# Half-size products in another order, channels split into chunks 0, 2 and 1, 3, norm by halves, and scores on 32 by 64 tiles

## The chip, the cores and the metric

The kernel runs on one core of one Trainium2 chip. The time is that of the device in microseconds, from the start of the program to its end. Engines are named as in the profile: PE is TensorE's matmuls and PEld its weight loads, DVE is VectorE, ACT is ScalarE, POOL is GpSimd, and SP, ACT and POOL also issue DMA transfers.

## The reference

The input `x` holds eight images of 32 by 32 positions with 512 channels, in fp32. Two attention layers follow each other, each with a group norm ahead of it and a residual around it:

```python
# N = 1024 positions, C = 512 channels, for each of 8 images
x = x + L0(gn(x))      # gn: 32 groups of 16 channels, mean and variance over positions and group
x = x + L1(gn(x))

def L0(xn):            # 16 heads of 32 channels
    q, k, v = split(xn @ w_qkv)
    return softmax(q * 32**-0.5 @ k.T) @ v @ w_proj + b_proj

def L1(xn):            # 4 heads of 128 channels
    q, k, v = xn @ Wq * 128**-0.5, xn @ Wk, xn @ Wv
    return softmax(q @ k.T + relative_position_logits(q, pos_emb_w, pos_emb_h)) @ v @ Wo
```

## The kernel before

Activations lie transposed in SBUF: a block has 128 partitions, four chunks of 128 channels (`CC` = 4) and 1024 positions, which are worked on in two halves of 512 (`NB`). A chunk is `xT[cc]`.

**Projections by seven products.** Each 512 by 512 projection is computed as a 2 by 2 block product with seven half-size products instead of eight (the Winograd form of Strassen's scheme). The activations' quarters are a11, a12 (first 512 positions), a21, a22 (last 512); the channels are cut into chunks 0, 1 (a11, a21) and 2, 3 (a12, a22). `forms` (L320) makes the four sums of quarters on DVE: s1 = a21 + a22, s2 = s1 - a11, a11 - a21 (in place of a21) and s4 = a12 - s2. The weights' quarters and sums are cut alike: `quarter` (L120), `Matrix.add_up` (L131, sums at L142, stored in DRAM). `seven` (L337) runs the products of one unit, half of the output channels, in the order P1, P6, P2, P5, P7, P3, P4 (indices 0, 5, 1, 4, 6, 2, 3 of `ORDER`, L161, which also sets the order in which `Stream` fetches weights). They add up in three PSUM banks, x, y and z; P1 and P7 are copied out by ACT as `p1` and `p7`, `a` (L368) and `b` (L376) are sums that DVE makes between two products into y, and a sink then makes the four results: `Plain` writes them, `Onto` adds them to the residual. Every product is issued by `by_columns` (L301), four matmuls of 32 output columns side by side. Unit u gives output chunks u and u + 2.

**Group norm.** `statistics` (L238) gathers mean and variance of a chunk on DVE into the tile `mv`; `group_norm` (L250) takes all four chunks at once: a 32 by 32 transpose, group averages, deviations, and back, about nine small DVE operations (L256 to L281), a power by POOL for 1/sqrt (L285), and then four DVE passes over the chunks (L288), in place. `put_away` stores the chunks as they were ahead of the norm, and `fetch` brings them back for the residual.

**Attention of layer 0** (`attention_0`): steps over groups of four heads m, halves of queries h and blocks of 128 keys j. A front (L525) computes the scores of four heads of 32 channels, each 128 keys by 512 queries, on four row tiles of TensorE, into the four banks of the one PSUM tile `ps`; ACT takes the exponential into `e` (L533, two buffers). A back (L544) adds the values, four heads side by side in columns, and DVE sums the `e` of all key blocks (L553, L555). `finish` and `normalise` divide by the row sums (DVE L493 to L509, POOL L513).

```python
for r in range(HB):                       # L522: HB = 4 heads
    rows = slice(r * D0, (r + 1) * D0)    # D0 = 32
    nc.tensor.matmul(ps[:, r, :], k[m][rows, j * P : (j + 1) * P],
                     q[m][rows, h * NB : (h + 1) * NB], start=True, stop=True)
```

**Attention of layer 1** (`attention_1`): steps over heads, halves and key blocks, with 128 by 128 matmuls (L640, L641, L652); heads in the order 0, 1, 2, 3.

**Order of the work.** The images overlap. While layer 0's attention of image b runs, `side_by_side` puts between its steps the output projection of layer 0 of image b - 1 (`after_0`, weights `w_p`), that of layer 1 of image b - 2 (`after_1`, `w_o`) with the norm of image b - 1 woven in, layer 1's projections (`second`, `w_q`, `w_k`, `w_v`) and attention of image b - 1, and the projections of image b + 1. Where there is no image b - 2, in the second round, the norm has nothing beside it: it is given `ALONE` steps, in which attention goes on by itself. A planner sets the final order of instructions on each engine from there. `load_first` brings the first image by matmul transposes; the weights' sums of the first three matrices are made around it.

Of the kernel before, what the change touches and what calls it, by code (L numbers as in the profile page):

```python
# [27 lines left out]
def quick_path(  # L28
# [68 lines left out]
    neg_half = consts.tile([P, CC], F32, tag="neg_half", name="neg_half")  # L97
# [22 lines left out]
    def quarter(w, i):  # L120
        k, n = i // 10 - 1, i % 10 - 1
        return w[:, k * HC : (k + 1) * HC, n * HN : (n + 1) * HN]

    class Matrix:

# [6 lines left out]
        def add_up(self, engine, queue, store, keep=False):  # L132

            t = block(f"prep_{self.name}")
            whole = t[:, : CC // 2, :].rearrange("p a (b n) -> p (a b) n", n=NB)
            sums = t[:, CC // 2 :, :].rearrange("p a (b c n) -> p (a b) c n", c=HC, n=HN)
            queue.dma_start(whole, self.w)
# [23 lines left out]
    ORDER = [0, 5, 1, 4, 6, 2, 3]  # L161
# [47 lines left out]
    def put_away(xT, name):  # L209
        kept = []  # L210
        for cc in range(CC):
            d = dram.tile([P, N], F32, tag="kept", name=f"d_{name}_{cc}", bufs=4 * CC)
            nc.sync.dma_start(d, xT[cc])
            kept.append(d)
        return kept
# [21 lines left out]
    def statistics(st, xT, cc, name):  # L237

        if "mv" not in st:
            st["mv"] = small.tile([P, 32], F32, tag="mv", name=f"mv_{name}", bufs=2)  # L240
            nc.gpsimd.memset(st["mv"], 0.0)
        s = small.tile([P, NH, 6], F32, tag="st", name=f"st_{name}_{cc}", bufs=2)
        for h in range(NH):
            nc.vector.bn_stats(s[:, h, :], xT[cc][:, h * NB : (h + 1) * NB])
        nc.vector.bn_aggr(
            st["mv"][:, : 2 * CC].rearrange("p (s c) -> p c s", c=CC)[:, cc, :],
# [3 lines left out]
    def group_norm(st, xT, name, after=None):  # L250

        mv = st.pop("mv")
# [16 lines left out]
        with tc.issue_after(after().ins) if after is not None else nullcontext():  # L269
# [9 lines left out]
        mean = back[:, 0, :CC]  # L279
        var = small.tile([P, CC], F32, tag="var", name=f"var_{name}")  # L280
        nc.vector.scalar_tensor_tensor(  # L281
            var, back[:, 0, CC : 2 * CC], GN_EPS, back[:, 1, :CC], op0=ALU.add, op1=ALU.add
        )
        rstd = small.tile([P, CC], F32, tag="rstd", name=f"rstd_{name}")
        nc.gpsimd.tensor_tensor(rstd, var, neg_half, op=ALU.pow)  # L285
        yield 0
        for cc in range(CC):
            nc.vector.tensor_scalar(  # L288
                xT[cc],
                xT[cc],  # L290
                mean[:, cc : cc + 1],
                rstd[:, cc : cc + 1],
                op0=ALU.subtract,
                op1=ALU.mult,
            )
            if cc % 2:
                yield 0
# [22 lines left out]
    def forms(x, name):  # L320


        a11, a12 = x[:, :HC, :NB], x[:, HC:, :NB]
        a21, a22 = x[:, :HC, NB:], x[:, HC:, NB:]
        s1, s2, s4 = [
            mem.tile([P, HC, NB], F32, tag=f"form{i}", name=f"f{i}_{name}", bufs=1) for i in (1, 2, 4)
        ]
        nc.vector.tensor_add(s1, a21, a22)  # L328
        nc.vector.tensor_sub(s2, s1, a11)  # L329
        nc.vector.tensor_sub(a21, a11, a21)  # L330
        nc.vector.tensor_sub(s4, a12, s2)
        return [a11, a12, s4, a22, s1, s2, a21]
# [4 lines left out]
    def seven(fs, u, rows, sink, name, hook=None):  # L337
# [26 lines left out]
        yield HC  # L364
        y = bank(f"y_{name}")
# [13 lines left out]
        z = bank(f"z_{name}")  # L379
        product(z, 6, True)  # L380
        p7 = snapshot("e1", f"p7_{name}")
        nc.scalar.copy(p7, z)  # L382
# [3 lines left out]
        if hook is not None:  # L386
            hook()
        yield HC
        product(z, 3, False)
        sink.c21(z, a)  # L390
        sink.c22(b, p7)
# [76 lines left out]
    def project_rows(fs, m, y, name, hook=None):  # L468

        for u in range(2):  # L470
# [11 lines left out]
                hook if u else None,  # L482
# [32 lines left out]
    def attention_0(q, k, v, b):  # L515
# [4 lines left out]
        def front(m, h, j):  # L520
            name = f"0_{b}_{m}_{h}_{j}"
            ps = psum.tile([P, HB, NB], F32, tag="ps", name=f"ps_{name}", bufs=1)  # L522
            for r in range(HB):
                rows = slice(r * D0, (r + 1) * D0)
                nc.tensor.matmul(  # L525
                    ps[:, r, :],
                    k[m][rows, j * P : (j + 1) * P],
                    q[m][rows, h * NB : (h + 1) * NB],
                    start=True,
                    stop=True,  # L530
                )
# [98 lines left out]
    def attention_1(q, k, v, posT, b):  # L630

        steps = [(h, c, j) for h in range(H1) for c in range(NH) for j in range(NT)]
# [56 lines left out]
    def load(b, st):  # L689
# [17 lines left out]
        st["kept"] = put_away(xT, f"0_{b}")  # L707
        yield from group_norm(st, xT, f"0_{b}")
# [3 lines left out]
    def load_first(st):  # L712

        rows = block("x_rows", [P, NT, C])
        for t in range(NT):
            queue = nc.scalar if t % 2 else nc.sync
            queue.dma_start(rows[:, t, :], xf[0, t * P : (t + 1) * P, :])
        x = block("x0T_0")
        xT = chunks(x)
        for h in range(NH):  # L720
# [13 lines left out]
            for cc in range(CC):  # L734
                part = xT[cc][:, h * NB : (h + 1) * NB]
                if h == 0 or cc % 2:
# [3 lines left out]
        for cc in (1, 0, 3, 2):  # L740
            statistics(st, xT, cc, "0_0")
        st["kept"] = put_away(xT, "0_0")
        run(group_norm(st, xT, "0_0"))
# [18 lines left out]
    def before_0(b, st, hook=None):  # L762
# [10 lines left out]
    def after_0(b, st, hook=None):  # L773
# [3 lines left out]
        xT = fetch(st["kept"], x)  # L777
        for u in range(2):
# [3 lines left out]
                fs, u, False, Onto(halves(xT, u), bias), f"wp_{b}_{u}", hook if u else None  # L782
# [4 lines left out]
    def norm_1(b, st, after=None):  # L787
        xT = chunks(st["x1"])
        st["kept"] = put_away(xT, f"1_{b}")
        yield from group_norm(st, xT, f"1_{b}", after)  # L790

    def second(b, st):
# [12 lines left out]
            keys_and_values, position_logits(q, posT, b), 2, len(ORDER), (0, 1, 2)  # L805
# [3 lines left out]
    def forms_1(b, st):  # L809
        st["ao1"] = forms(st["ao"], f"ao1_{b}")  # L810

    def after_1(b, st, hook=None):

        if "ao1" not in st:
            forms_1(b, st)
        fs = st.pop("ao1")
        xT = fetch(st["kept"], block(f"x2T_{b}"))
# [637 lines left out]
```

## Time and profile before

| | |
|---|---|
| time, median of 3 runs | 3914.23 us (3910.26 to 3914.39) |
| profiled run, span | 3913.0 us, mean clock of TensorE 0.993 |
| PE idle before its first products (11.4 to 24.8 us) | 13.4 us |
| ACT exponential of four heads, L533 | 512 of 1.88 us |
| DVE row sums of layer 0, L555 and L553 | 384 of 2.31 us, 64 of 2.74 us |
| DVE sum of quarters (one of four of `forms`) | 1.2 us, more beside POOL |
| POOL multiply of `normalise`, L513 | 128 of 1.67 us |

In the profile, a line of a group gives the source line, engine and operation, the tile written and the tiles read, the shape (for TensorE first rows times columns of the array in use), how often, then busy time and mean duration, then the idle time of the engine ahead of these instructions and what ended it. TensorE's matmuls overlap, so their durations don't add up to time; what counts is from one group's start to the next.

### The profile page before, as it was taken

The numbers are of one execution on the slowest core, as the hardware profiler recorded it, in microseconds if no ns is written. First come the engines' busy times: TensorE is split into PE (matmuls) and PEld (weight loads), VectorE is DVE, ScalarE is ACT, GpSimd is POOL, SyncE is SP. The second block draws the span as 40 slices with busy tenths as digits, with TensorE's granted clock in tenths as the row PEclk, the third lists the DMA queues.
The fourth block names the chain that finished last, engine by engine and source line by source line (L and its number), as shares of the span: only waits on it lengthen the run. The fifth ranks groups of instructions, "written<-read, shape, count | busy, mean of one in ns | idle before, by whom it ended". The sixth has DMA issues, their size and how long they took to land. (4 is left out here: it accounts for less than half of the span.)

```text
span 3913.0 us, 71616 instructions
## 1 busy us (share of the span) xinstructions
PE 3820.3 (98%) x30370; PEld 1414.5 (36%) x30370; DVE 2518.9 (64%) x2905; ACT 1726.1 (44%) x1767; POOL 620.7 (16%) x400
## 2 busy tenths in 40 slices
PE   7999899999999999999999999999999999999998
PEld 3222244232443234432343323433234332344353
DVE  5777675576745867468664686656865568754544
ACT  2554553445434454344544445344453445543132
POOL 1341001121101211012111121111200112011101
PEclk8999999999999999999999999999999999999999
DMA  5231120133201322023120241103311122110401
GB/s 168 74 108 50 41 60 3 39 117 70 59 5 63 106 56 55 12 90 84 44 54 17 91 94 39 44 24 97 88 44 32 30 91 68 32 63 18 124 17 23
DMA packets 482952, 234.21 MB, mean 60 GB/s; under 512 B 269600, under 2 KB 461376, under 8 KB 481600
## 3 DMA queue, kind: packets, MB, share of 16 engines
q1 hardware_dynamic: 470464, 212.69, 20.0%
q0 software_dynamic: 2608, 13.70, 0.9%
q8 instruction: 242, 3.96, 0.4%
q10 hardware_dynamic: 9552, 3.15, 0.4%
q14 instruction: 86, 0.70, 0.1%
HBM read 170.72 MB, written 58.72 MB: 59 GB/s over the span
## 5 line engine op out<-in xcount | busy, mean ns | idle before, releaser
L533 ACT ACTIVATE e<-ps 128x2048 f32<-128x2048 f32 x512 | 962.1, 1879 | 844.8 <-PE ps L525 650.1
L555 DVE TENSOR_TENSOR es<-es,e 128x2048 f32<-128x2048 f32 x384 | 888.7, 2314 | 405.6 <-ACT e L533 403.5
L525 PE MATMUL ps<-q,k 32*128 32x512 f32 x4096 | 591.3, 642 | 33.7 <-ACT e L533 33.6
L643 ACT ACTIVATE e<-ps 128x512 f32<-128x512 f32 x512 | 305.9, 598 | 585.8 <-PE ps L641 549.4
L544 PE MATMUL acc<-e,v 128*32 128x512 f32 x4096 | 549.5, 608 | 0.4 <-ACT su L491 0.4
L640 PE MATMUL ps<-q,k 128*128 128x512 f32 x1024 | 523.6, 593 | 0.4 <-DVE posT L626 0.4
L652 PE MATMUL acc<-e,v 128*128 128x512 f32 x1024 | 521.9, 592 | 0.0
L513 POOL TENSOR_TENSOR q<-q,su 128x512 f32<-128x512 f32 x128 | 214.2, 1673 | 1568.2 <-DVE su L509 1567.5
L663 DVE TENSOR_TENSOR es<-es,e 128x512 f32<-128x512 f32 x384 | 291.7, 760 | 264.5 <-ACT e L643 263.2
L641 PE MATMUL ps<-posT,sel 128*128 128x512 f32 x512 | 406.7, 794 | 0.0
L525 PEld LDWEIGHTS ps<-q,k 32*128 32x128 f32 x4096 | 161.7, 183 | 429.7 <-ACT e L533 212.9
L640 PEld LDWEIGHTS ps<-q,k 128*128 128x128 f32 x1024 | 193.6, 190 | 246.2 <-issue 240.6
L652 PEld LDWEIGHTS acc<-e,v 128*128 128x128 f32 x1024 | 193.1, 189 | 146.7 <-issue 105.0
L544 PEld LDWEIGHTS acc<-e,v 128*32 128x32 f32 x4096 | 81.6, 108 | 386.6 <-issue 342.1
L553 DVE TENSOR_TENSOR es<-e,e 128x2048 f32<-128x2048 f32 x64 | 175.2, 2737 | 39.1 <-ACT e L533 39.1
L493 DVE STREAM_TRANSPOSE tu<-su 128x512 f32<-128x512 f32 x128 | 90.7, 708 | 135.8 <-ACT su L491 135.6
L641 PEld LDWEIGHTS ps<-posT,sel 128*128 128x128 f32 x512 | 97.3, 190 | 122.5 <-issue 122.5
L491 ACT COPY su<-sums 128x512 f32<-128x512 f32 x128 | 75.1, 586 | 149.9 <-PE sums L565 81.8
L661 DVE TENSOR_TENSOR es<-e,e 128x512 f32<-128x512 f32 x64 | 44.2, 690 | 145.7 <-ACT e L643 145.7
L626 DVE TENSOR_TENSOR posT<-pp,posT 32x512 fp32r<-32x512 f32 x128 | 111.8, 874 | 32.2 <-ACT posT L621 30.8
L417 POOL TENSOR_TENSOR k<-b_k,p_k 128x512 f32<-128x512 f32 x32 | 50.3, 1572 | 477.8 <-ACT p_k L382 477.8
L621 ACT CAST posT<-pp 32x512 fp32r<-32x512 f32 x128 | 106.0, 828 | 45.3 <-PE pp L608 44.2
(193 smaller groups left out, 4516.0 us busy)
## 6 DMA issues: line engine op xcount, KB each, us to landing
w_qkv<-ws_qkv SPq DMA_DIRECT2D x168, 128.0 KB, 2.4
d<-x0T SPq DMA_DIRECT2D x32, 512.0 KB, 3.6
x1T<-d SPq DMA_DIRECT2D x32, 512.0 KB, 4.9
d<-x1T SPq DMA_DIRECT2D x32, 512.0 KB, 3.6
x2T<-d SPq DMA_DIRECT2D x32, 512.0 KB, 6.0
w_qkv<-in_L_conv_w_qkv SPq DMA_DIRECT2D x126, 128.0 KB, 2.2
out<-ot SPq DMA_DIRECT2D x240, 64.0 KB, 2.0
xs<-in_x SPq DMA_DIRECT2D x224, 64.0 KB, 2.4
```

The source lines that it names most:

```text
L513: nc.gpsimd.tensor_tensor(dst, dst, su, op=ALU.mult)
L525: nc.tensor.matmul(ps[:, r, :], k[m][rows, j * P : (j + 1) * P], q[m][rows, h * NB : (h + 1) * NB], start=True, stop=True,)
L533: nc.scalar.activation(e, ps, AF.Exp, scale=D0 ** -0.5)
L544: nc.tensor.matmul(acc[r * D0 : (r + 1) * D0, :], v[:, j, c0 : c0 + D0], e[:, r, :], start=(j == 0), stop=(j == NT - 1),)
L553: nc.vector.tensor_add(state["esum"], state["first"], e)
L555: nc.vector.tensor_add(state["esum"], state["esum"], e)
L626: nc.vector.tensor_sub(rest, logits, greater)
L640: nc.tensor.matmul(ps, k[h][:, keys], q[:, h, queries], start=True, stop=False)
L641: nc.tensor.matmul(ps, sel_flat[:, keys], posT[:, h, queries], start=False, stop=True)
L643: nc.scalar.activation(e, ps, AF.Exp, scale=1.0 / math.sqrt(D1))
L652: nc.tensor.matmul(acc, v[:, j, h * D1 : (h + 1) * D1], e, start=(j == 0), stop=(j == NT - 1),)
L663: nc.vector.tensor_add(state["esum"], state["esum"], e)
```

## The change

Five things are changed together.

1. The channels are cut into chunks 0, 2 and 1, 3, which are the chunks that the two units of a projection finish, so that a half of the next operand is whole after one unit. Layer 1's heads run in the order 0, 2, 1, 3 to the same end.
2. The seven products run in the order P1, P7, P6, P2, P5, P4, P3. P1 needs a11, P7 the sum s3 = a11 - a21, both of half 0; sums are made in three steps (`forms_in_parts`), which callers can spread over two hooks.
3. Group norm runs by halves, twice for two chunks, and the callers weave each half in by itself.
4. The first weights are fetched ahead of the first image's other transfers, DVE and ACT share the first copies otherwise, and six matmuls whose result nobody reads run before the first norm.
5. Layer 0's scores run on eight tiles of 32 rows by 64 columns instead of four of 32 by 128.

It is meant to let TensorE go on where it waited for a norm or a sum over all channels, and to shorten the weight loads ahead of the scores. The diff, cut to its core:

```diff
     def quarter(w, i):
         k, n = i // 10 - 1, i % 10 - 1
-        return w[:, k * HC : (k + 1) * HC, n * HN : (n + 1) * HN]
+        return w[:, k::2, n * HN : (n + 1) * HN]
...
-    ORDER = [0, 5, 1, 4, 6, 2, 3]
+    ORDER = [0, 6, 5, 1, 4, 3, 2]
...
-    def put_away(xT, name):
+    def put_away(st, xT, half, name):
-        for cc in range(CC):
+        for cc in (half, half + 2):
...
-    def group_norm(st, xT, name, after=None):
-        mv = st.pop("mv")
+    def group_norm(st, xT, half, name, after=None):
+        name = f"{name}_{half}"
+        mv = st.pop(f"mv{half}")
...
-        for cc in range(CC):
+        for c in range(HC):
             nc.vector.tensor_scalar(
-                xT[cc],
-                xT[cc],
+                xT[half + 2 * c],
+                xT[half + 2 * c],
...
+    def forms_in_parts(x, name, got):
+        a11, a12 = x[:, 0::2, :NB], x[:, 1::2, :NB]
+        a21, a22 = x[:, 0::2, NB:], x[:, 1::2, NB:]
+        s3 = form(3)
+        nc.vector.tensor_sub(s3, a11, a21)
+        nc.vector.tensor_add(a21, a21, a22)
+        s2 = form(2)
+        nc.vector.tensor_sub(s2, a21, a11)
+        yield
+        s4 = form(4)
+        nc.vector.tensor_sub(s4, a12, s2)
+        got += [a11, a12, s4, a22, a21, s2, s3]
...
         nc.scalar.copy(p1, x)
         yield HC
+        z = bank(f"z_{name}")
+        product(z, 6, True)
+        p7 = snapshot("e1", f"p7_{name}")
+        nc.scalar.copy(p7, z)
+        yield HC
         y = bank(f"y_{name}")
         product(y, 5, True)
...
-        z = bank(f"z_{name}")
-        product(z, 6, True)
-        p7 = snapshot("e1", f"p7_{name}")
-        nc.scalar.copy(p7, z)
+        product(z, 3, False)
+        sink.c21(z, a)
+        sink.c22(b, p7)
+        next(hook, None)
         yield HC
         product(y, 2, False)
         sink.c12(y, p1)
-        if hook is not None:
-            hook()
-        yield HC
-        product(z, 3, False)
-        sink.c21(z, a)
-        sink.c22(b, p7)
+        next(hook, None)
         yield HC
...
-            for r in range(HB):
-                rows = slice(r * D0, (r + 1) * D0)
-                nc.tensor.matmul(
-                    ps[:, r, :],
-                    k[m][rows, j * P : (j + 1) * P],
+            for i in range(2):
+                some = slice(64 * i, 64 * i + 64)
+                for r in range(HB):
+                    rows = slice(r * D0, (r + 1) * D0)
+                    nc.tensor.matmul(
+                        ps[some, r, :],
+                        k[m][rows, j * P + 64 * i : j * P + 64 * i + 64],
...
-        steps = [(h, c, j) for h in range(H1) for c in range(NH) for j in range(NT)]
+        steps = [(h, c, j) for h in (0, 2, 1, 3) for c in range(NH) for j in range(NT)]
...
+        WV0.fetch(nc.sync)
...
-                if h == 0 or cc % 2:
+                if h == 0 or cc >= 2:
                     nc.scalar.copy(part, banks[cc])
...
+        idle = psum.tile([P, CC, NB], F32, tag="ps", name="idle", bufs=1)
+        for t in range(6):
+            nc.tensor.matmul(idle[:, t % CC, :], ident, rows[:, t, :], start=True, stop=True)
+        for half in range(2):
+            for cc in (half, half + 2):
+                statistics(st, xT, cc, "0_0")
+            put_away(st, xT, half, "0_0")
+            run(group_norm(st, xT, half, "0_0"))
...
         yield from woven(
-            keys_and_values, position_logits(q, posT, b), 2, len(ORDER), (0, 1, 2)
+            keys_and_values, position_logits(q, posT, b), 4, len(ORDER), (0, 1, 2)
         )
...
             if past is not None:
-                rest.append(woven(later(after_1, b - 2, past), norm, 3, 3))
+                norms = chain(*(norm_1(b - 1, last, half, lambda: half_done[0]) for half in range(2)))
+                rest.append(after_0(b - 1, last, forms_1(b - 2, past)))
+                rest.append(woven(later(after_1, b - 2, past), norms, 4, 2))
                 total += PRODUCT
             else:
-                rest.append(chain([ALONE], (cost + ALONE for cost in norm), marked()))
-                total += 4 * ALONE
+                norms = [norm_1(b - 1, last, half) for half in range(2)]
+                rest.append(woven(after_0(b - 1, last), norms[0], len(ORDER) + 3, 2))
+                rest.append(chain([ALONE], (cost + ALONE for cost in norms[1]), marked()))
+                total += 3 * ALONE
```

## The prediction

> **What bounds the kernel now.** I read the busy line of the page first, then the costliest groups, then the timeline of one steady stretch, then every place where TensorE stood still.
>
> ```profile
> PE 3820.3 (98%) x30370; PEld 1414.5 (36%) x30370; DVE 2518.9 (64%) x2905; ACT 1726.1 (44%) x1767; POOL 620.7 (16%) x400
> ...
> L525 PE MATMUL ps<-q,k 32*128 32x512 f32 x4096 | 591.3, 642 | 33.7 <-ACT e L533 33.6
> ...
> L544 PE MATMUL acc<-e,v 128*32 128x512 f32 x4096 | 549.5, 608 | 0.4 <-ACT su L491 0.4
> ...
> L525 PEld LDWEIGHTS ps<-q,k 32*128 32x128 f32 x4096 | 161.7, 183 | 429.7 <-ACT e L533 212.9
> ...
> L544 PEld LDWEIGHTS acc<-e,v 128*32 128x32 f32 x4096 | 81.6, 108 | 386.6 <-issue 342.1
> ```
> TensorE is busy 98% of the span, so time comes only from shorter work on TensorE or from the 93 us in which it is idle (11 of them after its last matmul). Lines 525 and 544 do equally many products of equal size, yet 525 takes 42 us more. The timeline says why:
>
> ```profile
> 1006.03 0.31 PEld L525 LDWEIGHTS ps<-q,k 32*128 32x128 f32 x8 [0.41 <-issue]
> 1006.03 1.14 PE L525 MATMUL ps<-q,k 32*128 32x512 f32 x8
> ...
> 1007.10 0.16 PEld L544 LDWEIGHTS acc<-e,v 128*32 128x32 f32 x8 [0.76 <-issue]
> 1007.10 1.07 PE L544 MATMUL acc<-e,v 128*32 128x512 f32 x8
> ...
> 1007.98 1.91 PE L308 MATMUL x_v<-w_v,x1T 128*32 128x256 f32 x32
> ```
> A score group (line 525, eight records for four fp32 products side by side) holds TensorE 1.07 us from its start to the next start; the value group after it 0.88. Both stream the same. A score matmul takes 692 ns in the first pass and 587 in the second (median and least of that tile): the first waits 105 ns for weights that no earlier group let it load. In the value group of this window it is 617 against 592: 25 ns.
>
> The gaps, from the timeline:
>
> ```profile
> 24.79 1.08 PE L308 MATMUL x_v<-prep_qkv,x0T 128*32 128x256 f32 x8 [13.41 <-DVE x0T L288]
> ...
> 347.57 3.08 PE L308 MATMUL y_wp<-f_ao,w_p 128*32 128x512 f32 x16 [3.46 <-DVE f_ao L329]
> ...
> 401.89 2.09 PE L525 MATMUL ps<-q,k 32*128 32x512 f32 x8 [7.57 <-ACT e L533]
> ...
> 884.82 1.92 PE L308 MATMUL y_wo<-f_ao,w_o 128*32 128x512 f32 x16 [1.37 <-DVE a_wo L368]
> ...
> 3877.30 3.43 PE L308 MATMUL y_wo<-f_ao,w_o 128*32 128x512 f32 x16 [3.15 <-DVE f_ao L329]
> ```
> In brackets stands how long TensorE was idle before it and who ended that. The first waits for the norm, the second and the last for VectorE's sums, the third for an exponential whose buffer VectorE freed late; the fourth recurs once per image (at 884.82, 1359.34, 1833.91: period 474.5 us). In 347 and 3877 sixteen matmuls take 3.1 and 3.4 us instead of 1.9: after the gap the clock was halved for 3.41 us.
>
> **What the Trainium skill says.** "TensorE: Matmul & The Clock Gate", LDWEIGHTS: a load takes columns / 1.2 ns, whatever the rows; that is 107, 53 and 27 ns for 128, 64 and 32 columns. The trace agrees at both ends (105 and 25 ns of stall; loads of 183 and 108 ns). Same page, HAM clock gate: an idle window of about 3.4 us halves the clock; the trace has steps of 3.41 us. "TensorEngine Tiling (Array Packing)", Key Properties: tiles run independently, and a change of the tiling mode drains the array; agrees, as about 0.1 us is lost at the change into and out of line 525. Its list of configurations has 32x64 with eight tiles; no instruction before has that shape.
>
> **The change part by part.**
>
> *Scores on 32 by 64 tiles.* Four products of 128 columns become eight of 64: same streaming, same two mode changes. The exposed load falls from 107 to 53 ns. Against it, eight pairs of load and matmul have to be issued instead of four; in the trace four overlapping matmuls of 692 ns cover 0.71 us, so each starts some 7 ns after the one before it, and four more put the last one 27 ns later. Net 27 ns less per group (estimate). There are 4096/8 = 512 groups: **-14 us**. Bounds: -27 us (issue hidden) and, if the second four had to wait behind the first four, their full 854 ns each, +437 us.
>
> *Order of the seven products, and which sums they need.* P1 and P7 need half 0 alone (a11, and s3 = a11 - a21); before, P6 came second and waited for two sums over both halves. At 347, chunks 0 and 2 are final long before the last head's normalising, so P1 and P7 (1.7 us each) run where the gap was; P6 then waits for two sums of 1.2 us after the last multiply by GpSimd, which leaves some 0.7 us. Saved: 3.46 - 0.7 + half of 3.41 us of halved clock = **-4.5**. At the end, P1, P7 and P2 need nothing of the last half of the last head: gaps of 0.75 and 3.15 and 1.7 us of clock go (-5.6), and after the last product one transposed block has to leave instead of two (0.7 us a transpose, about 2 us of output packets): **-7.5**.
>
> *Norm by halves, image 0.* Before, from 389 to 417 us seven score rounds run without a product beside them, each waiting 1.0 us for its exponential, one 7.57 us, with 6.83 us of halved clock: some 15 us lost (4 x 1.0 + 7.57 + 3.4). Half 0 is now normed inside the projection, and the last chain ends in two chunk passes (0.8 us each) instead of four, with a row-sum addition between them. In the built program's order four rounds stand bare. I leave 5 us: **-10**.
>
> *Norm by halves, images 1 to 6.* A second chain: nine small VectorE operations (864.83 to 867.10: 2.3 us) and one more wait for GpSimd's power (1.5 us). Behind it in the queue stand the row sums, which free the exponentials' buffers, and the `a` and `b` sums that the products wait for. From 860 to 905 us VectorE is busy 42.3 of 45 us, so this is not hidden for certain. Bounds per image: -2.2 (today's two bubbles of 1.37 and 0.8 to 1.1 vanish) to +3.8 (all exposed). I take +0.5, six times: **+3**.
>
> *The start.* Fewer statistics stand before the first norm (four passes of 0.64 us and two small ones less), the weights land earlier (0.4 MB/us, behind 2 MB of rows), and six idle matmuls delay the halved clock. But the built order puts VectorE's four subtractions for WQ0 (0.65 us each) into the first chain and WK0's ahead of s3, which before came after all sums. Adding up by the trace's durations I get P1 at 25.4 instead of 24.8 us, P7 at 29 and P6 at 36; by 36 us 3.2 products are done against 3.3: **0** (-4 to +3).
>
> *The rest.* Snapshots, a sum in place, head order 0, 2, 1, 3, dictionary of stored chunks: same operations and bytes. The second half's tail in GpSimd (1.3 to 1.6 us) is now followed by a product; nothing waits for it. Last images (3224 to 3300, 8 us of gaps, VectorE full): **-1**.
>
> Sum: -14 - 4.5 - 7.5 - 10 + 3 + 0 - 1 = -34, so 3914 - 34 = **3880 us**.
>
> **Rivals.**
> - *All of it pays*: 53 ns per group (-27) and the image bubbles vanish (-13): -27 - 23 - 13 = 3851 us. For it: the issue of four matmuls is only 20 ns. Against: the last tile has to drain.
> - *VectorE becomes the bound* where the output projection runs: 3.8 us for each of six images (+23), hiding what the groups save (0 left), while the one-time gains (-23) stay: 3914, no change. For it: 94% busy there. Against: those stretches are a tenth of an image, and the groups elsewhere still shrink.
> - *The eight tiles do not fully overlap*: two tiles share each row group, and the second load waits for the first and its drain: +107 ns per group, +55 us; with -23 + 3 that is **3949 us, slower**. For it: no trace here shows row and column tiling together. Against: in 128*32 four column tiles overlap wholly, in 32*128 four row tiles do.
> - *Serial*: 3914 + 437 - 23 = 4328 us.
>
> **Numbers.** Forecast 0.52, all pays 0.15, VectorE bound 0.17, partial overlap 0.12, serial 0.04. The third case falls on both sides of no change (0.07, 0.05, 0.05), some of the forecast's spread reaches it, so faster 0.74, same 0.07, slower 0.19. The range 3848 to 3922 leaves out the serial case, nearly all of partial overlap and a little of the best.
>
> **What would show it.** A score group with first passes near 640 ns, loads near 131 ns (between 108 and 183) and about 1.04 us to the next start; no y_wp gap near 347; at most four bare rounds near 400; an image period near 473 us. The period shows VectorE as the bound if it stays at 474.5 with more gaps before y_wo. A score group of 1.2 us or more, or of 1.9, would make the forecast wrong.

## The result, and the profile after

The changed kernel takes **3945.3 us** (median of 4 runs, 3941.8 to 3948.5), the kernel before 3913.3 (4 runs beside them): ratio 1.0083, 95% interval 1.0065 to 1.0100. Slower by 32 us; forecast was 3880.

The busy line of the page and the two groups that the prediction set against each other (busy us, mean ns; idle just before and who ended it):

```profile
PE 3830.9 (97%) x34478; PEld 1365.6 (35%) x34478; DVE 2552.0 (65%) x3049; ACT 1724.0 (44%) x1767; POOL 556.8 (14%) x432
...
L545 PE MATMUL ps<-q,k 32*64 32x512 f32 x8192 | 578.6, 618 | 47.9 <-ACT e L553 47.8
...
L564 PE MATMUL acc<-e,v 128*32 128x512 f32 x4096 | 552.1, 611 | 0.0
...
L545 PEld LDWEIGHTS ps<-q,k 32*64 32x64 f32 x8192 | 120.2, 130 | 442.9 <-ACT e L553 220.9
```
The score groups (now line 545) did shrink: 578.6 us against 591.3, loads of 130 ns against 183. But their idle time before them rose from 33.7 to 47.9 us, all ended by the exponential. One score group and its value group in the timeline (start, us, engine, operation):

```profile
1004.82 1.11 PE L545 MATMUL ps<-q,k 32*64 32x512 f32 x16
...
1005.86 1.07 PE L564 MATMUL acc<-e,v 128*32 128x512 f32 x8
```
1.04 us from start to start, where before it was 1.07. All eight tiles overlap: their first passes start within 0.05 us of each other and take 638 ns, second ones 587 (medians). So neither rival that let the tiles overlap partly or not at all was right. That the time landed 4 us from one of them (3949) is luck.

The gaps, from the timeline (in brackets how long TensorE stood, and for whom):

```profile
23.51 3.64 PE L314 MATMUL x_v<-prep_qkv,x0T 128*32 128x256 f32 x32 [6.67 <-issue]
31.55 3.44 PE L314 MATMUL z_v<-prep_qkv,f_xn 128*32 128x256 f32 x32 [4.39 <-DVE var L288]
...
349.24 1.92 PE L314 MATMUL y_wp<-f_ao,w_p 128*32 128x512 f32 x16 [1.01 <-DVE f_ao L340]
...
395.64 1.28 PE L545 MATMUL ps<-q,k 32*64 32x512 f32 x16 [2.32 <-ACT e L553]
...
882.17 2.02 PE L545 MATMUL ps<-q,k 32*64 32x512 f32 x16 [3.50 <-ACT e L553]
...
3912.24 3.57 PE L314 MATMUL y_wo<-f_ao,w_o 128*32 128x512 f32 x16 [2.41 <-DVE f_ao L340]
```
The gap near 347 fell from 3.46 to 1.01 us and no halved clock follows it any more, the 7.57 near 402 fell to 2.32, the last from 3.15 to 2.41. New is the 3.50 us at 882.17, which returns at 1362.71, 1843.31, 2323.85 and 2804.37: once per image, and the period is now 480.6 us. The matmuls behind it take 2.02 us instead of 1.11: the trace records a halved clock there for 3.41 us (at 881 for 6.83).

To see where the time went I timed both kernels by the same marks, the first product of each projection. WP is the first attention's output projection, WO the second's; image 7 is the last image (the expectations below call its second attention, in the loop's last round, "image 8"). us, from the traces; "tiles alone" and "best version" are two of the experiments below:

| stretch | before | after | tiles alone | best version |
|---|---|---|---|---|
| start to image 0's WP | 340.9 | 342.5 | 338.6 | 335.6 |
| to image 1's WP | 468.1 | 460.3 | 466.9 | 457.6 |
| five periods to image 6's WP, each | 474.6 | 480.6 | 473.2 | 473.2 |
| to image 7's WP | 419.8 | 417.3 | 417.2 | 417.1 |
| to image 7's WO (no first attention beside) | 267.6 | 281.4 | 267.9 | 267.7 |
| WO to the last matmul | 32.7 | 30.9 | 32.7 | 30.6 |

The loss has two places: 6.0 us in each of five periods (+30) and 13.7 us after image 7's WP. The gains (image 0 -7.8, last rounds -2.5, end -1.8) are there too, but small. In both places of the loss TensorE stands longer, and the clock is halved more often behind the waits: in a period it stands 7.5 us instead of 2.5 and has 4.1 us of halved clock instead of none (means of five), after image 7's WP 13.0 us instead of 6.2 and 13.7 us of halved clock instead of none. If half of the halved clock is time lost (an estimate, from sixteen matmuls that take 3.4 us for 1.9), that is 7.1 us per period, of which the tiles give 1.4 back, and 13.6 us at the end.

### The profile page after: what moved, and what is told of

It reads as the page before. It is cut to its first block, busy times and chain, and to the rows that moved or that the text cites. A ratio compares the mean times of both kernels' runs of the same rounds, so it can differ in the third digit from the quotient of the medians.

```text
span 3946.5 us, 79983 instructions
## 1 busy us (share of the span) xinstructions
PE 3830.9 (97%) x34478; PEld 1365.6 (35%) x34478; DVE 2552.0 (65%) x3049; ACT 1724.0 (44%) x1767; POOL 556.8 (14%) x432
## 4 chain that ended last, share of the span: by engine, by line
PE 79%; DVE 12%; ACT 3%; issue 3%; DMA 1%; POOL 1%; SPq 0%; DVEq 0%; ACTq 0%; POOLq 0%
PE acc L672 11%; PE ps L545 11%; PE ps L660 11%; PE acc L564 9%; PE y_k L314 4%; PE y_q L314 4%; PE y_v L314 4%; DVE es L575 4%; PE ps L661 3%; PE z_v L314 3%; PE z_k L314 3%; PE x_k L314 2%; PE x_q L314 2%; PE z_q L314 2%; PE x_v L314 2%
## 5 line engine op out<-in xcount | busy, mean ns | idle before, releaser
L545 PE MATMUL ps<-q,k 32*64 32x512 f32 x8192 | 578.6, 618 | 47.9 <-ACT e L553 47.8
L683 DVE TENSOR_TENSOR es<-es,e 128x512 f32<-128x512 f32 x384 | 282.2, 735 | 259.3 <-ACT e L663 257.9
L530 POOL TENSOR_TENSOR q<-q,su 128x512 f32<-128x512 f32 x128 | 200.3, 1565 | 1509.5 <-DVE su L526 1461.9
L545 PEld LDWEIGHTS ps<-q,k 32*64 32x64 f32 x8192 | 120.2, 130 | 442.9 <-ACT e L553 220.9
L434 POOL TENSOR_TENSOR v<-b_v,p_v 128x512 f32<-128x512 f32 x32 | 42.9, 1341 | 394.5 <-DVE b_v L398 388.6
```

The source lines that it names most:

```text
L530: nc.gpsimd.tensor_tensor(dst, dst, su, op=ALU.mult)
L545: nc.tensor.matmul(ps[some, r, :], k[m][rows, j * P + 64 * i : j * P + 64 * i + 64], q[m][rows, h * NB : (h + 1) * NB], start=True, stop=True,
L683: nc.vector.tensor_add(state["esum"], state["esum"], e)
```

## What stands in VectorE's queue at the new gap

The timeline of the changed kernel, VectorE and those who wait for it, ahead of the gap at 1362.71:

```profile
1352.04 1.88 DVE L852 STREAM_TRANSPOSE ot<-x2T 128x512 f32<-128x512 f32 x3
...
1353.85 0.15 DVE L281 TENSOR_TENSOR turned<-turned,avg 128x32 f32<-128x32 f32 x1
...
1354.97 0.16 DVE L288 SCALAR_TENSOR_TENSOR var<-back 128x2 f32<-128x2 f32 x1
1355.28 0.69 POOL L292 TENSOR_TENSOR rstd<-var,neg_half 128x2 f32<-128x2 f32 x1 [8.12 <-DVE var L288]
...
1356.00 2.49 DVE L295 TENSOR_SCALAR x1T<-x1T,back,rstd 128x1024 f32<-128x1024 f32 x2 [0.87 <-POOL rstd L292]
...
1358.41 4.67 DVE L575 TENSOR_TENSOR es<-es,e 128x2048 f32<-128x2048 f32 x2
...
1360.78 1.88 ACT L553 ACTIVATE e<-ps 128x2048 f32<-128x2048 f32 x1 [6.35 <-DVE es L575]
...
1362.71 2.02 PE L545 MATMUL ps<-q,k 32*64 32x512 f32 x16 [3.51 <-ACT e L553]
```
and the same place in the kernel before:

```profile
1352.22 1.90 DVE L823 STREAM_TRANSPOSE ot<-x2T 128x512 f32<-128x512 f32 x3
...
1354.03 4.65 DVE L555 TENSOR_TENSOR es<-es,e 128x2048 f32<-128x2048 f32 x2
```
Read it upward from the gap. The score group waited for PSUM, which the exponential had to read; the exponential waited 6.35 us for one of the two buffers `e0`; the buffer is freed by the row sum `es`. The exponential that the first of these two row sums adds had run from 1347.37 to 1349.25. But ahead of the row sum in VectorE's queue stood, behind the transposes, the rest of the second norm chain (1353.85 to 1355.13), 0.87 us of waiting for GpSimd's power, and half 1's two passes (2.49 us). Before, the row sums came right behind the transposes. The Trainium skill, "PSUM — Partial Sum Buffer", Engine vs sequencer instructions, says that VectorE's and ScalarE's queues are strict FIFO; the trace agrees: a row sum whose inputs were there stood still while VectorE waited 0.87 us for another operation's input.

My theory at this point: this second chain makes the loss. The rivals: the new order of products, and the tiles.

## Experiments

Line numbers move by a few lines from kernel to kernel. "Period" is the mean of five, from WP to WP.

**The tiles, alone and undone.**

```diff
@@ kernel before: attention_0.front, one product of 128 columns becomes two of 64
-            for r in range(HB):
+            for i in range(2):
+                for r in range(HB):
...
```


> The kernel before with one thing of the change: scores on 32 by 64 tiles, eight matmuls in place of four. Theory of the norm (the tiles pay as forecast, the loss is VectorE's queue at the second norm chain): 512 groups x 27 ns, so 3914 - 14 = 3900 us (3895 to 3904), image period 474.5 - 1.8 = 472.7. Rival (shorter score groups only hand the time on to waits, so the tiles have a part in the loss): 3910 to 3920, the gaps before the scores and before y_wo longer by what the groups save.


Measured: 3903.0 us beside 3912.6, ratio 0.9976 (0.9970 to 0.9983), period 473.2.

The same edit backwards, in the changed kernel:

> The changed kernel with the scores back on 32 by 128 tiles. If the tiles pay 27 ns per group in the changed kernel too: 3945 + 14 = 3959 us, period 480.6 + 1.8 = 482.4. If VectorE's queue sets the time where they shrink: 3945 to 3950.


Measured: 3953.4 us, period 481.9. The tiles pay 8 to 10 us by the medians in the two kernels (13.7 between the profiled executions of before and tiles alone, 3913.0 and 3899.3). They have no part in the loss.

**One chain, and the old order: two first tries.**

```diff
@@ changed kernel: images 1 to 7
-norms = chain(*(norm_1(b - 1, last, half, lambda: half_done[0]) for half in range(2)))
+norms = norm_1(b - 1, last, "w", lambda: half_done[0])   # chunks 0, 2, 1, 3 in one chain
-rest.append(woven(later(after_1, b - 2, past), norms, 4, 2))
+rest.append(woven(later(after_1, b - 2, past), norms, 3, 3))
```


> The changed kernel, but images 1 to 7 norm all four chunks of the first attention's result in one chain as before (in the order 0, 2, 1, 3, woven into the output projection at steps 3, 6, 9 instead of 4, 6, 8, 10); image 0 keeps its halves, the products keep their new order. Theory of the second chain in VectorE's queue: the gap of 3.51 us with its halved clock, the gap of 1.44 and most of the one before the sums go, period 474 (473 to 476) instead of 480.6, so 3945 - 6 x 6.5 = 3906 us (3900 to 3915). Rival, order of the products (gaps follow from sums and banks in the new order): period stays 479 to 481, 3938 to 3946.


Measured: 3937.3 us, period 478.7: neither number, though near the rival's. Step 3 of the new order is P2, which comes ahead of P5 and its sum `b`; the chain thus stood earlier than before the change and right in front of another row sum, with a gap of 3.63 us there.

```diff
@@ changed kernel
-ORDER = [0, 6, 5, 1, 4, 3, 2]
+ORDER = [0, 5, 1, 4, 6, 2, 3]
...
```


> The changed kernel with its products back in the order P1, P6, P2, P5, P7, P3, P4 (halves, norm by halves and tiles stay). Theory of the second chain: the periods keep 479 to 482; only image 8's second attention, where nothing runs beside the products and waits of 12.8 us stand against 5.6 before, gets back some 7 to 12 us, and the start and the gap at 347 lose what the order gave (1 to 5): 3936 to 3944 us. Rival, order of the products: period falls to 475 or less, 3905 to 3915.


Measured: 3941.8 us, period 478.2, image 7 from WP to WO 277.5 (281.4). The total is as expected, but the periods gave 2.4 us (480.6 to 478.2), which my theory did not allow for.

**One chain at the step where it was.** 4, 7, 10 instead of 3, 6, 9:

> As the run with one norm chain, but woven into the output projection at steps 4, 7, 10 instead of 3, 6, 9, so that with the new order of products the chain again stands behind the sum b of the product P5, as it did before (at step 3 it stood two products earlier, right after unit 1's statistics, ahead of a row sum). Theory, that what costs is what stands in VectorE's queue ahead of a row sum: the gap of 3.63 us before a score group goes, period 474 to 476, 3910 to 3920 us. Rival, the new order of the products itself: period stays at 478 or more, 3935 to 3942.


Measured: 3930.6 us, period 477.9. The gap of 3.5 us is gone, as expected, but total and period are neither theory's: a row sum makes another gap, the line `sums` below. So one chain gives back 15 us of the 32, not all.

**Logits earlier, half 0 elsewhere.**

```diff
@@ changed kernel
-keys_and_values, position_logits(q, posT, b), 4, len(ORDER), (0, 1, 2)
+keys_and_values, position_logits(q, posT, b), 3, len(ORDER), (0, 1, 2)
```


> The changed kernel with the position logits woven in from step 3 instead of 4 (step 2, as before, can't be had with the new order: the bank that the logits take is free only after P2). If the late logits cause image 8's loss (VectorE's differences for the logits stand ahead of the sum that frees the next unit's bank): image 8 from its output projection to its last one (281.4 us in the changed kernel, 267.7 before) falls to 272 to 276, total 3937 to 3941, periods 479 to 481. Rival, the order itself: 280 to 282, 3943 to 3947.


Measured: 3976.2 us, period 485.4, image 7 281.4. Neither: 31 us worse, with more waits in the second attention's projections; which bank or sum makes them I did not settle.

```diff
@@ changed kernel
-rest.append(after_0(b - 1, last, forms_1(b - 2, past)))
-rest.append(woven(later(after_1, b - 2, past), norms, 4, 2))
+rest.append(woven(after_0(b - 1, last, forms_1(b - 2, past)), norms[0], len(ORDER) + 3, 2))
+rest.append(woven(later(after_1, b - 2, past), norms[1], 4, 3))
```


> The changed kernel, but for images 1 to 7 half 0's norm is woven into the projection WP (as it is for image 0), and half 1's into the output projection at steps 4, 7. The number of operations is the same, only the queue ahead of the row sums changes. Theory of the place in the queue: the 3.51 us gap goes, 3915 to 3930 us, period 475 to 478. Rival, the second chain's work as such (VectorE full in the output projection): 3940 to 3950, period 479 to 482.


Measured: 3955.9 us, period 482.6. The 3.51 us gap went and one of 4.06 us came, in WP ahead of P3, for the sum `b`. Another place in the queue was not better, and the result is worse than either number expected.

**A staircase from tiles to the change.** The next runs split the change into steps. Each of the last three steps differs in one thing; the two above them are bundles. First everything undone but tiles, start, chunks 0, 2 and 1, 3, and image 0's halves (with the forms in parts and the next image's norm by halves still in):

> The changed kernel with products in the old order, position logits from step 2 as before, and one norm chain at 3, 6, 9 for images 1 to 7: of the change are left the tiles, chunks 0, 2 and 1, 3, image 0's norm by halves, the forms in parts and the start. If order and second chain together make the loss: periods 473 to 474, image 8 268 us, in all 3913 - 10 (tiles, as measured alone) - 6 (image 0) = 3897 us (3890 to 3903). Rival, something else of the change (forms in parts, stored chunks by halves, order of heads): periods 476 or more, 3912 or more.


Measured: 3910.2 us, ratio 0.9997 (0.9988 to 1.0006), period 474.6: better by 35 us than the change, 13 worse than expected, with a period between the two expected. Then the forms made as before and the next image's norm in one chain:

```diff
-s3 = form(3)
-nc.vector.tensor_sub(s3, a11, a21)
-nc.vector.tensor_add(a21, a21, a22)
...
+nc.vector.tensor_add(s1, a21, a22)
+nc.vector.tensor_sub(s2, s1, a11)
+nc.vector.tensor_sub(a21, a11, a21)
...
```


> As the run with tiles and image 0 only, but the forms are made as before (sum s1 in a buffer, a11 - a21 last and in place), all four at the first hook, and the next image's norm (woven into the second attention) is one chain too. There the period was 474.6 where the tiles alone have 473.1, so 1.5 us per image is left to explain. Theory, the forms in parts (and the second chain of the next image's norm) account for it: period 473.0 to 473.5, total 3910 - 9 = 3901 us. Rival, chunks by halves or the order of heads: period 474.3 or more, 3908 to 3911.


Measured: 3905.7 us, ratio 0.9980, period 473.1: the period is the expected one, the total 5 us above the expected (image 0's WP to image 1's is longer, 466.3 us against 462.9). And upward, the second norm chain put back, with the old order and the logits at step 2:

> The changed kernel with the products in the old order, as in the run of that name, and also the position logits woven in from step 2 as before (the second norm chain stays). Theory that the later logits, which the new order forces, cost in image 8: image 8 falls from 277.5 us to some 269 (267.6 where one chain is also undone), total 3941 - 9 = 3932 us; periods stay at 477 to 479, as the second chain is still there (2.7 us of it). Rival, the chain costs in image 8 too: image 8 stays at 275 or more, 3938 to 3942.


Measured: 3931.5 us, ratio 1.0049 (1.0033 to 1.0066), period 477.2, image 7 270.8. The total is within 1 us of the expected. The staircase (medians; total, period, and image 7 from WP to WO):

| kernel | us | step | period | image 7 |
|---|---|---|---|---|
| before | 3912 to 3913 | | 474.6 | 267.6 |
| + tiles | 3903.0 | -9.6 | 473.2 | 267.9 |
| + start, chunks 0, 2 and 1, 3, image 0's halves | 3905.7 | +2.7 | 473.1 | 267.6 |
| + forms in parts, next image's norm by halves | 3910.2 | +4.5 | 474.6 | 267.6 |
| + second norm chain, images 1 to 7 | 3931.5 | **+21.3** | 477.2 | 270.8 |
| + logits from step 4 | 3941.8 | **+10.3** | 478.2 | 277.5 |
| + order P1, P7, P6, P2, P5, P4, P3 (= after) | 3945.3 | +3.5 | 480.6 | 281.4 |

The 95% intervals of these totals reach 3 to 7 us to each side, so the steps of 2.7, 4.5 and 3.5 us are not shown by the totals; for them the periods and stretches of the traces have to speak. The chain's step is clear of that, and between the profiled executions it is 18.5 us. The logits' step was tried twice, here and on the best version below.

**The chain's work or its place?** Here the chain's nine small operations, its power and the wait are left out, and half 1 takes half 0's mean and deviation, with its passes where they were:

```diff
@@ changed kernel: group_norm, half 1 of images 1 to 7
+short = half == 1 and after is not None
...
+if short:
+    mean, rstd = st.pop("stats0")
+else:
...
```


> The changed kernel, but for images 1 to 7 half 1 is normed with half 0's mean and deviation: its nine small VectorE operations, its power on GpSimd and the wait for it are left out; statistics and passes stay, at the same steps. Theory, the chain's work and wait are what costs (2.9 us per image by the runs with one chain and with two): 3945 - 20 = 3925 us (3922 to 3930), period 477.7. Rival, it is the order of the passes by halves: 3938 to 3946, period 479.5 or more.


Measured: 3928.8 us, period 477.5, within 4 us of the expected. Its timeline, at the same place:

```profile
1350.93 1.50 DVE L301 TENSOR_SCALAR x1T<-x1T,back,rstd 128x1024 f32<-128x1024 f32 x2
1352.34 4.68 DVE L581 TENSOR_TENSOR es<-es,e 128x2048 f32<-128x2048 f32 x2
...
1356.65 1.12 PE L551 MATMUL ps<-q,k 32*64 32x512 f32 x16 [0.37 <-ACT e L559]
```
The same two passes now wait for nobody, the row sums begin 1.3 us after the end of the transposes instead of 4.5, and the gap is 0.37 us. So the chain and what it brings with it, not the passes by halves, cost the 3 us per image. Two things in this were not in the theory. Of the 3.2 us in the queue 1.0 is the passes themselves, which take 1.50 us here and took 2.49 in the changed kernel: there an addition by GpSimd, which here runs at 1347.79, stood behind the power in GpSimd's queue and ran beside them (1355.94 to 1357.21). And of the 3.1 us of a period only 1.8 is standing less (7.5 to 5.7 us); the rest goes with the halved clock, which falls from 4.1 to 0.7 us a period.

**Forms held back.** The run with one chain at 4, 7, 10 had this ahead of its gap (row sum last in its head, line 580):

```profile
1358.34 1.22 DVE L343 TENSOR_TENSOR x1T<-x1T 128x1024 f32<-128x1024 f32 x1
...
1358.50 2.19 POOL L449 TENSOR_TENSOR x2T<-x2T,a_wo 128x512 f32<-128x512 f32 x1 [9.69 <-DVE a_wo L395]
...
1359.59 2.19 DVE L345 TENSOR_TENSOR f_xn<-x1T 128x1024 f32<-128x1024 f32 x1
...
1361.70 2.28 DVE L580 TENSOR_TENSOR es<-es,e 128x2048 f32<-128x2048 f32 x1
...
1364.12 1.06 PE L590 MATMUL sums<-es,ones 128*32 128x512 f32 x8 [2.01 <-DVE es L580]
```
The forms for the second attention stand ahead of the row sum that TensorE waits for. With the new order they can come that early: by the code, the buffer of a11 - a21 is last read by P7, now second of seven.

```diff
-nc.vector.tensor_sub(s3, a11, a21)
+with tc.issue_after(after.ins) if after is not None else nullcontext():
+    nc.vector.tensor_sub(s3, a11, a21)
...
-fs = forms(st.pop("x1"), f"xn1_{b}")
+fs = forms(st.pop("x1"), f"xn1_{b}", half_done[0] if b else None)
```
`half_done[0]` is the sum `b` of WO's unit 1.

> As the run with one norm chain woven in later (new order kept, period 477.9), but the first of the next forms (a11 - a21 for the second attention's projections) is held behind the sum b of P5 in the output projection's unit 1. In VectorE's queue three forms of together 4.6 us then stand behind the last row sum of that head instead of ahead of it; nothing else moves. Theory: the new order frees the buffer of P7's form earlier, so the forms come earlier in the queue, and TensorE waits 2.0 us for that row sum and then runs 3.4 us at half clock: period 477.9 - 3.7 = 474.2 (473.5 to 475.5), total 3931 - 22 = 3909 us (3904 to 3916). Rival, the loss moves to another place in the queue: period 477 or more, 3927 to 3933.


Measured: 3928.0 us, period 477.9: the rival. The `sums` gap is gone, and this one has come in its place:

```profile
1374.27 1.88 ACT L559 ACTIVATE e<-ps 128x2048 f32<-128x2048 f32 x1 [6.57 <-DVE es L579]
...
1376.20 1.12 PE L551 MATMUL ps<-q,k 32*64 32x512 f32 x16 [2.31 <-ACT e L559]
```
Two of the forms now stand ahead of the next head's first row sum. Moving work within this stage of VectorE's queue moves the wait along; taking work out of it (the chain) shortens it.

**Work moved to GpSimd.** Is then each us taken off VectorE a us of time?

```diff
 def c22(self, b, p7):
-    self.add(1, 1, p7)
+    if self.bias is None:
+        self.gather(1, 1, p7)      # nc.gpsimd
+        self.then(1, 1)
...
```
In the changed kernel:


> The changed kernel, but the output projection's sum C22 (p7 onto the stored chunk, all of it in SBUF, 0.69 us on VectorE, twice per image) is done by GpSimd (1.28 us). Theory that VectorE is full in this stage, so that each us taken off it is a us of time: 1.4 us less per image, for seven images -8 to -10, so 3936 us and period 479.2. Rival, only the place of the chain counts (the two sums stand behind the row sum that TensorE waits for): 3943 to 3947.


Measured: 3944.6 us, period 480.4: no gain. On the version with image 0's halves only:


> The version with tiles and image 0's halves only, with the same sum on GpSimd. VectorE is busy 15.8 of 16 us where TensorE's two gaps (1.0 and 1.4 us per image) lie. Theory of the full VectorE: up to 1.4 us per image, 3901 - 8 = 3893 us (3891 to 3897), period 471.7. Rival: 3899 to 3903, period 473.1, since the gaps end with an exponential or a sum that doesn't stand behind C22.


Measured: 3912.2 us, ratio 1.0003 (0.9994 to 1.0011), 11 us slower than its base by the medians (6 between the profiled executions); period 474.2. Neither theory allowed for that. The pages' busy lines say part of it: sixteen sums of 0.69 us (11 us) left VectorE, yet it is busy 2530.2 us against 2527.1 in the base (2553.7 against 2552.0 in the changed kernel). So the other VectorE operations grew by as much and a little more. The lines of **Forms held back** show such a case: a form of 1024 elements takes 1.22 us at 1358.34 and 2.19 us at 1359.59, where GpSimd's addition runs until 1360.69. The skill, "SBUF — State Buffer", SBUF: two separate sides, says that VectorE with two inputs from SBUF and GpSimd take a shared pair of ports under an exclusive lock, for a whole instruction; both times agree with it: GpSimd's addition, begun at 1358.50, ends 1.13 us after the form of 1358.34 does, and the form of 1359.59 ends 1.09 us after the addition. So these two runs do not answer the question: in sum no time was taken off VectorE. Why the second one's period grew by 1.0 and image 7's stretch by 5.6 us I did not settle.

**A version that beats both.** Image 0's halves with the tiles and nothing else:

> The kernel before with the tiles, the chunks 0, 2 and 1, 3, and image 0's norm by halves, and nothing else of the change (start, forms, order, logits and norm chains of images 1 to 7 as before; the order of heads and the stored chunks by halves stay). Tiles alone measured 3903; image 0's stretch from its projection to image 1's was 468.1 us before, 466.9 with tiles alone and 460 to 463 with the halves. If that gain is independent of the rest: 3903 - 4 = 3899 us (3895 to 3902), the best version so far. Rival (the gain needs the new order, whose P1 and P7 take half 0): 3902 to 3905.


Measured: 3900.8 us, ratio 0.9968 (0.9956 to 0.9979). As expected in total, but the stretch from image 0's WP to image 1's is 466.3 us (466.9 with the tiles alone), so by themselves image 0's halves give almost nothing. With the forms in parts and the next image's norm by halves it was 462.9 in the old order too; the new order is not the only thing that helps them. Next, the new order where no second chain and no logits are near, in image 0's WP and in the last WO (on the base with GpSimd's sum):

> As the version with tiles, image 0's halves and C22 on GpSimd, and the new order of products (with a11 - a21 made first) in two places only: image 0's projection WP and the last image's output projection. The order's own gain: the gap of 3.5 us at 345 falls to 1.0 and half of 3.4 us of halved clock goes (-4), the end -2: 6 us below the run with C22 on GpSimd that is its base. Rival (a mixed order makes the weights' loads for the next unit wait): no gain, or slower.


Measured: 3902.7 us, 9.5 below its base (3912.2). The same without GpSimd's sum:

> Tiles, image 0's halves, and the new order in image 0's projection WP and the last output projection; the output projection's sums all on VectorE again. If the gains add: 3901 - 9.5 = 3891 us (3888 to 3896), period 473.1. Rival (the order's gain was partly recovery of what GpSimd's sum had cost): 3896 to 3900.


Measured: **3891.6 us**, ratio 0.9953 (0.9936 to 0.9969). Start to image 1's WP is 793 us against 805 for its twin without the order (3 of these 12 us lie ahead of image 0's WP, where the two do the same), the end 30.6 against 32.7.

And this version with the logits from step 4:

> The same with the position logits woven in from step 4 instead of 2, and no second norm chain. If the later logits cost by themselves: image 8 +6 to +8 us (267.7 to 275), periods +0.4, so 9 to 10 us above its twin. Rival, they cost only behind a second chain: 0 to 3 us above it.


Measured: 3903.8 us, 12 above its twin; image 7 275.8, period 474.2. The late logits cost by themselves. How, the timeline of the changed kernel shows, in image 7's second attention:

```profile
3722.16 1.76 DVE L646 TENSOR_TENSOR posT<-pp,posT 32x512 fp32r<-32x512 f32 x2 [0.91 <-ACT posT L641]
...
3723.95 0.69 DVE L427 TENSOR_TENSOR k<-y_k,p_k 128x512 f32<-128x512 f32 x1
...
3724.70 1.92 PE L314 MATMUL z_k<-f_xn,w_k 128*32 128x512 f32 x16 [0.84 <-DVE k L427]
...
3771.51 0.47 PE L661 MATMUL ps<-posT,sel 128*128 128x512 f32 x1 [1.85 <-DVE posT L646]
```
Two steps later in the unit, two of the four logit differences stand ahead of the unit's last sum, and that sum frees the bank for the next unit's P7; the last differences come too late for the scores that need them (1.85 us). In the best version, with the logits from step 2, all four were done by then, and the next unit's first product waits 0.24 us:

```profile
3664.95 3.58 DVE L695 TENSOR_TENSOR posT<-pp,posT 32x512 fp32r<-32x512 f32 x4 [0.96 <-ACT posT L690]
...
3668.63 1.92 PE L319 MATMUL x_k<-x1T,w_k 128*32 128x512 f32 x16 [0.24 <-PE z_k L319]
```
Four such waits stand in image 7's second attention: 0.84, 0.90, 1.84 and 1.85 us in the changed kernel, 0.80, 0.90, 1.80 and 1.86 in the best version with the logits from step 4, and 0.24 to 0.31 in its twin. That is 4.3 us of the 8.1 between the twins there; 6.8 us of halved clock, which the twin does not have, go with the rest.

## Why the prediction was wrong

- **Norm by halves, images 1 to 6, +0.5 per image:** the step that failed most. The operations were counted rightly (2.3 us and a wait), and the bound of +3.8 for "all exposed" was close; I took +0.5, because VectorE has 6% idle there and today's bubbles might vanish. By the staircase it is 3.0 us for each of seven images (+21.3; 2.6 by the periods), and leaving the operations out gives 16.5 back. Three things were missing: images 1 to 7 are seven, not six; the clock, which is halved behind the longer waits and which I had priced at 347 but not here; and the passes that ran beside GpSimd.
- **"Same operations and bytes", -1:** the second failure. The diff moves the logits from step 2 to 4, and I did not price it; it is +10.3 (12 on the best version). The forms in parts were not priced either (+4.5 with the next image's norm by halves). The order was priced in two places where it pays, not in the periods, where it costs 2.4 us each.
- **Start, 0 (-4 to +3):** too low. +1.6 up to image 0's WP, 3.9 above tiles alone. The thirteen kernels with the changed start come to that point at 341.6 to 347.9 us, the seven with the old one at 335.2 to 340.9; the version with image 0's halves and nothing else has 338.7, and 345.5 with the changed start. P1 came at 23.5 us (25.4 worked out), P7 at 31.6 (29), P6 at 37.8 (36).
- **Score groups, -14:** right in mechanism and in each figure of the group; 8 to 10 us by the medians, 13.7 between the profiled executions; the period gave 1.4 us of 1.8 (64 groups x 28 ns). One reading was too kind: the loads take 183, 130 and 108 ns for 128, 64 and 32 columns, so only their differences (53 and 22) fit the 107, 53 and 27 that were worked out, not the durations.
- **Order at 347, -4.5:** right. The gap is 2.45 us shorter and 3.41 us of halved clock are gone, which makes 4.2 (half of the clock counted).
- **Norm by halves for image 0, -10:** much too large. The stretch from image 0's WP to image 1's gained 7.8, of which the tiles have 1.2 and the gap at 347 4.2. The bare score rounds remained, with waits of 2.3, 1.7 and 1.6 us. Halves without the rest leave the stretch at 466.3; with the order in this place (best version) it is 457.6.
- **End, -7.5:** -1.8, and nothing off the output that follows. P6 still waits 4.9 us from the start of GpSimd's multiply, as before: the first sum takes 2.27 us and not the 1.2 that I had put in, since GpSimd's next addition runs beside it. Only P7's 1.7 us fill part of that.
- **Rivals:** "VectorE becomes the bound" was right on the place and on the size for the chain (+23 worked out). It came out at 3914, 31 us too low, for want of the logits (10) and because it kept the one-time gains of 23 us, most of which did not come. Whether each us on VectorE counted, as it says, is not shown: holding forms back took no work away, and moving a sum took none in the end. The chances have a slip: for slower 0.05 + 0.12 + 0.04 is 0.21, not 0.19, and the 0.02 that go to no change come from faster (0.72).

Left open in part: the order's 2.4 us per period. All nine kernels with the new order throughout wait for the sum `b` in WP in each of the five periods, 1.0 us in the changed kernel; none of the other eleven does. From the old order to the new one TensorE stands 1.6 us longer per period in all (5.9 to 7.5) and has 1.4 us more of halved clock; which operation in VectorE's queue makes the rest of the waits is not shown, and holding the forms took away one wait and brought another.

## What to carry to other kernels

Ask of an operation added to an in-order queue what is *ready* behind it, not how idle the engine is: some 2 us of small operations and a wait, put ahead of a row sum that frees a buffer, came out as 3 us of time on an engine that is busy 65% overall, part of it by a halved clock behind the wait. Price every number that a diff moves, a weaving step too: one digit cost 10 us. And apply a reordering only where the wait that it removes exists: in two places the new order brought 9 us, and in each period it cost 2.4.

## What the runs showed of the hardware

- Eight tiles of 32 by 64 overlap wholly: 16 records in 1.11 us, first passes of 638 ns.
- A form on VectorE grows from 1.22 to 2.19 us beside a GpSimd addition, and two norm passes from 1.50 to 2.49. So work moved to GpSimd comes back in other operations: 11 us of sums left VectorE, and its busy time rose by 3.1 us.
- No length of wait tells in these traces whether the clock halves. With one chain at 4, 7, 10 TensorE stood 2.01 us up to 1364.12 and the clock was halved for 3.41 us from 1365.43; the kernel before stood 2.88 us up to 3667.81, and no halved clock followed. The window of about 3.4 us, with which the prediction worked, is thus not a bound for a single wait.
